# Two attentions and two feed-forward stages on one core: the first attention's last slab in pairs of slots, FFN products in the last batch's slots, a lead of three tiles

## The chip, the cores and the metric

The kernel runs on one core of a Trainium2 chip. The metric is the device time of one execution in microseconds (us). It is shown beside one profiled execution, whose trace gives every instruction's start and length on the engines: PE (TensorE, matmuls; PEld its weight loads), DVE (VectorE), ACT (ScalarE), POOL (GpSimd), and the DMA queues, of which SP (SyncE) issues most. TensorE's clock can be granted at less than full speed; the profile gives the granted share.

## The reference

For 4 batches of 256 tokens of width 256, with a context of 1601 tokens of width 128 per batch:

```
x = x + tanh(g_xattn[0]) * L0_xattn(layernorm(x), ctx)   # 16 heads of 16, q and k normed
x = x + tanh(g_ffn[0])   * L0_ffn(layernorm(x))          # shared expert + 8 of 16 routed
x = x + tanh(g_xattn[1]) * L1_xattn(layernorm(x), ctx)   # 16 heads of 128, 8 key heads
x = x + tanh(g_ffn[1])   * L1_ffn(layernorm(x))          # ternary weights, SiLU gate
```

The two parts that the change touches:

```
def L0_xattn(x, y):          # the last 16 context tokens attend apart and are added
    q = ln(x @ Wq + bq); k = ln(y_main @ Wk + bk); v = y_main @ Wv + bv
    ctx = softmax(q k^T / 4) v + softmax(q k_dca^T / 4) v_dca
    return ctx @ Wo + bo

def L0_ffn(x2):
    shared = x2 @ sw1.T * relu(x2 @ swg.T)**2 @ sw2.T
    xl = x2 @ Wdown.T                                     # the latent, width 64
    for e in range(16):
        ye = xl @ rw1[e].T * relu(xl @ rwg[e].T)**2 @ rw2[e].T
        acc += w_dense[:, e:e+1] * ye
    return shared + acc @ Wup.T
```

## The kernel before

The four stages run one after another; matmul outputs are [channels, tokens] or [keys, queries]. Within a stage a helper (`keep_order`) fixes every engine's order to the order in which the program records it, so the recorded order is the queue.

**First attention (lines 284 to 1247).** It works in *slabs* of one batch and four heads: 16 slabs, `u` from 0 to 15, four per batch. The four heads of a slab lie in four groups of 32 rows, so that a score matmul with 32 rows of contraction uses a quarter of PE's rows, and matmuls on different row groups run at the same time. A slab is cut into 14 *slots* (`SLOTS`): seven pairs of key tiles (the last has one tile), each once for the heads in row groups 0 and 1 and once for those in groups 2 and 3. A slot of `attend_tile` (L884) makes the scores of two heads for two key tiles (L894) into two PSUM banks, which ACT turns into exponentials (L904). After every odd slot `weigh` (L909, matmuls L918) multiplies the exponentials of two key tiles by the values.

Before a slab's scores its row maxima are needed. `greatest_tile` (L835) makes them from 14 tiles a slab: matmuls L849 into two banks of `ps_g`, DVE reductions L859 or L861. When the last of a slab's 14 is reduced, `shift` (L873 to L877) puts the maximum into the staged queries `qp`, and `turn_queries` (L803, transposes L807) turns them for the score matmuls. These tiles run ahead of the slots: one tile goes beside the scores in each slot, the list `ahead` starts one tile in front, and extra tiles at the slots in `CATCH_UP` (3, 5 and 7) bring the lead to four (`LEAD`). So the list ends in slot 205, and slots 206 to 223 have scores alone. The turn for the next slab is booked from slot 10 of a slab on, at odd slots in the first three batches and at even ones in the last.

PSUM has eight banks here: `ps_s` 3, `ps_g` 3, `ps_o` 1 (sums of `weigh`), `ps_m` 1. Everything else passes through `ps_m`: key and value projections, query projection, transposes, routing. `book` gives each such step a slot of its own, `chain` a row of slots, and `place` puts a step that needs no bank after a slot's work. Among them are the layernorm of the next batch (`plan_norm`, L1049; DVE L116 to L124, POOL L120), the projection, scaling and swap of the keys (`plan_keys`; the swap is three rounds of DMAs on SP, L643 to L649, for a pair of slabs), and in the last batch the routing of batches 0 to 2 (`route`, L203; matmuls L208 and L247).

**The opening loop (L1198 to L1215)** makes slab 0's maxima (seven steps `k`, two tiles each, four DVE reductions), beside the key projection of the second key set (steps 0 to 3, `key_project`: L522 into `ps_o`, activations L526 and L534), its roots (step 4: L557 into `ps_m`, DVE L564), and the value projection of batch 1, one pair of key tiles a step (`value_project`, L652: two matmuls L659, a copy by ACT L660).

**The end of the stage:** the last `weigh`, `take` (a copy by ACT), `put_heads` (transposes L940, DVE, POOL L949), `turn_heads` (L957), `out_project` (L965).

**First FFN (L1303 to L1480).** Tokens go in two halves of 512, two batches each. At its start `latent(0)` and `shared(0)` make the latent and the shared expert's products of the first half from `xnT` (`from_x`, matmuls L1383 with 256 columns; each 32-bit float matmul is two PE instructions). Then 32 experts follow (16 per half): `expert` (matmuls L1410, L1411, L1412 into `ps_v`, `ps_g`, `ps_w`), relu on ACT, products on DVE and POOL, `add_pair` (L1424). Between the experts stand other steps in `beside`: `latent(1)` at step 10 and `shared(1)` at step 13, and the preparation of the second attention. The slices of the tiles `scs` and `sq`, of 512 columns each, hold the results (`held`).

**Second attention and second FFN** follow (from L1487); the change leaves them as they are.

## Time and profile before

| | us |
|---|---|
| median of 3 runs (1486.24 to 1492.55) | 1489.6 |
| the profiled execution | 1492.74 |
| its span | 1491.0 |
| last matmul of `weigh` ends | 473.6 |
| first expert's matmul starts | 482.26 |
| first matmuls of the second attention on the chain | 583.45 |

Each row of the page's part 1 gives an engine's busy time, its share of the span and its instructions. The row of digits cuts the span in 40 slices of 37.3 us: PEclk is the clock that PE was granted in tenths, where 9 stands for 90% or more. Windows give, for a stretch of time, PE, PEld, DVE, ACT and POOL busy (with the count of instructions), then the granted clock, the DMA share and GB/s. The chain is the work that ended last, followed back from the end: start, length, engine, tile and line. Matmuls are pipelined, so lengths of single matmuls in the timeline overlap; the length of a group is what it took together.

Some further rows of the trace: the exponential L904 of 128 x 512 takes 571 ns on average, a reduction L859 624 ns and L861 621 ns. In all, PE waited 13.5 us for exponentials in the stretch from 88 to 440 us, and 2.8 us for the swap's DMA up to 90 us.

### The profile page before, as it was taken

To read this page: it belongs to the slowest core of one execution; us is meant where nothing else is said; L and a number is where in the kernel's file an instruction comes from. 1 tells how busy PE (TensorE), PEld (TensorE's weight loads), DVE (VectorE), ACT (ScalarE), POOL (GpSimd) and SP (SyncE) were. 2 spreads that over 40 slices of the span, in tenths; PEclk is the share of its full clock that TensorE was granted. 3 is DMA by queue.
4 is the path that set the end of the run, shared out by engine and by line. 5 is a ranking of instruction groups with operands and counts; after the bars stand their busy time and mean duration, and the time that the engine had idled before them with its cause. 6 is when DMAs were issued, how large, how long until landed. Compare 5 with 4: busy or idle time off the path is not lost.

```text
span 1491.0 us, 32194 instructions
## 1 busy us (share of the span) xinstructions
PE 1434.7 (96%) x12234; PEld 896.4 (60%) x12234; DVE 1081.6 (73%) x2556; ACT 802.9 (54%) x2055; POOL 641.5 (43%) x622
## 2 busy tenths in 40 slices
PE   7889999998999999799999999999999999999998
PEld 4455555555555444466666666666666666666677
DVE  6777787787761756877777777777877777877755
ACT  4467778687654344454444555444554444554433
POOL 4444463343321553444444444444444444445430
PEclk9799999999987999899999999999999999999999
DMA  5333422331212300000000000000000100000000
GB/s 136 45 53 65 65 48 32 56 57 35 62 44 62 134 1 1 2 9 10 16 16 16 9 10 16 16 9 9 10 17 9 23 9 16 10 2 2 2 1 29
DMA packets 63079, 43.47 MB, mean 29 GB/s; under 512 B 46474, under 2 KB 57100, under 8 KB 62796
## 3 DMA queue, kind: packets, MB, share of 16 engines
q1 hardware_dynamic: 48636, 39.66, 12.7%
q10 hardware_dynamic: 14288, 1.75, 0.7%
q8 instruction: 96, 1.57, 0.4%
q14 instruction: 59, 0.48, 0.1%
HBM read 32.67 MB, written 4.66 MB: 25 GB/s over the span
## 4 chain that ended last, share of the span: by engine, by line
PE 87%; DVE 5%; ACT 3%; POOL 2%; DMA 1%; issue 1%; SPq 0%; ACTq 0%; DVEq 0%; POOLq 0%
PE ps_o L1648 24%; PE ps_sc L1585 22%; PE ps_o L918 6%; PE ps_s L894 6%; PE ps_y L1666 4%; PE ps_m L1574 4%; PE ps_g L849 3%; PE ps_v L1410 2%; ACT e L904 2%; PE ps_m L659 1%; PE ps_m L522 1%; PE ps_a L1424 1%; DVE mxs L859 1%; PE ps_y L1826 1%; PE ps_g L1803 1%
## 5 line engine op out<-in xcount | busy, mean ns | idle before, releaser
L1635 POOL TENSOR_TENSOR pr<-pr,rs 128x1604 f32<-128x1604 f32 x128 | 364.0, 2866 | 443.6 <-DMA rs<-ws 379.1
L1648 PE MATMUL ps_o<-pT,cx 128*128 128x256 f32 x1664 | 372.0, 381 | 8.2 <-DVE pT L1641 8.2
L1592 DVE CUSTOM_DVE_ANT_0 pr<-ps_sc,mk 128x401 f32<-128x401 f32 x512 | 294.3, 576 | 92.9 <-PE ps_sc L1585 54.1
L1585 PE MATMUL ps_sc<-ctxT,qT 128*32 128x401 f32 x4096 | 359.5, 502 | 0.5 <-DVE nm L1592 0.5
L1600 ACT ACTIVATE pr<-pr,nm 128x401 f32<-128x401 f32 x512 | 321.2, 628 | 69.7 <-DVE nm L1592 69.0
L1648 PEld LDWEIGHTS ps_o<-pT,cx 128*128 128x128 f32 x1664 | 317.6, 191 | 52.8 <-DVE pT L1641 9.3
L904 ACT ACTIVATE e<-ps_s 128x512 f32<-128x512 f32 (+1 forms) x429 | 222.1, 571 | 103.0 <-PE ps_s L894 65.7
L859 DVE TENSOR_REDUCE mxs<-ps_g 128x1 f32<-128x454 f32 x372 | 216.8, 624 | 64.8 <-PE ps_s L894 40.0
L1585 PEld LDWEIGHTS ps_sc<-ctxT,qT 128*32 128x32 f32 x4096 | 126.2, 110 | 204.3 <-issue 118.3
L1641 DVE STREAM_TRANSPOSE pT<-pr 128x1664 f32<-128x1664 f32 x128 | 242.9, 1899 | 5.2 <-POOL pr L1635 5.2
L894 PE MATMUL ps_s<-qT,kS 32*128 32x256 f32 x1596 | 185.1, 319 | 16.0 <-ACT e L904 14.1
L894 PEld LDWEIGHTS ps_s<-qT,kS 32*128 32x128 f32 x1596 | 128.1, 192 | 95.1 <-ACT e L904 52.0
L849 PE MATMUL ps_g<-kS,qT 32*128 32x454 f32 (+1 forms) x960 | 160.1, 397 | 11.2 <-DVE mxs L861 4.3
L1617 ACT ACTIVATE ws<-ws 32x32 f32<-32x32 f32 x64 | 14.6, 228 | 201.5 <-DVE ws L1616 201.5
L918 PE MATMUL ps_o<-e,vp 128*32 128x256 f32 x1664 | 122.2, 409 | 0.0
L1658 ACT COPY ao<-ps_o 128x256 f32<-128x256 f32 x64 | 23.8, 372 | 151.5 <-PE ps_o L1648 136.4
L1600 ACT ACTIVATION_READ_ACCUMULATOR pr<-pr,nm 128x1 f32 x512 | 95.4, 186 | 0.0
L849 PEld LDWEIGHTS ps_g<-kS,qT 32*128 32x128 f32 x960 | 78.0, 188 | 18.4 <-DVE mxs L859 7.8
L1666 PE MATMUL ps_y<-vo,ao 128*128 128x256 f32 x256 | 72.2, 405 | 0.0
L1666 PEld LDWEIGHTS ps_y<-vo,ao 128*128 128x128 f32 x256 | 43.3, 189 | 43.9 <-ACT pr L1600 39.8
L918 PEld LDWEIGHTS ps_o<-e,vp 128*32 128x32 f32 x1664 | 44.9, 114 | 39.6 <-issue 14.7
L1614 DVE TENSOR_REDUCE low<-bq 32x8 f32<-32x32 f32 x64 | 12.4, 194 | 74.3 <-DMA bq<-nm 74.2
(346 smaller groups left out, 1632.3 us busy)
## 6 DMA issues: line engine op xcount, KB each, us to landing
scs<-by_row SPq DMA_DIRECT2D x56, 93.8 KB, 4.4
ctxT<-in_ctxT_dram SPq DMA_DIRECT2D x4, 800.5 KB, 8.2
held<-kS SPq DMA_DIRECT2D x32, 99.1 KB, 3.0
kS<-kS SPq DMA_DIRECT2D x32, 99.1 KB, 3.3
kS<-held SPq DMA_DIRECT2D x32, 99.1 KB, 3.6
ctx<-in_ctxT_dram SPq DMA_DIRECT2D x12, 200.0 KB, 4.2
kS<-in_L_xattn_Wq_dram SPq DMA_DIRECT2D x8, 256.0 KB, 5.0
wo<-in_L_xattn_Wo_dram SPq DMA_DIRECT2D x4, 512.0 KB, 4.7
```

The source lines that it names most:

```text
L849: nc.tensor.matmul(ps[:, m * w : (m + 1) * w], lhsT=part[rows, ii * P : (ii + 1) * P], rhs=kT[rows, n * CW0 : n * CW0 + w], start=part is ...
L859: nc.vector.tensor_reduce(mx[:, i, r + k, n : n + 1], ps[:, :w], AX.X, ALU.max)
L894: nc.tensor.matmul(ps[:, jj * S : (jj + 1) * S], lhsT=kT[rows, (j + jj) * P : (j + jj + 1) * P], rhs=part[rows], start=part is parts[0], s ...
L904: nc.scalar.activation(e[:, i, : nj * S], ps[:, : nj * S], AF.Exp)
L918: nc.tensor.matmul(summed[u][(r + k) * W : (r + k + 1) * W, :S], lhsT=vps[b % 2][:, t, h * VW : h * VW + W], rhs=made[u, j, r][:, k, jj * ...
L1585: nc.tensor.matmul(ps[i * TQ : (i + 1) * TQ, :KS], lhsT=queries[u][:, t * TQ : (t + 1) * TQ], rhs=ctxT[b][:, i * KS : (i + 1) * KS], start ...
L1592: nc.vector.tensor_tensor_reduce(out=prs[u % 3][:, t, :KS], in0=ps[:, :KS], in1=masks[b], scale=-1.0, scalar=3.0e38, op0=ALU.add, op1=ALU. ...
L1600: nc.scalar.activation(p, p, AF.Exp, bias=found[u][:, 0, t : t + 1], scale=-1.0, accum_out=found[u][:, 1, t : t + 1])
L1635: nc.gpsimd.tensor_tensor(p, p, bc_last(factors[:, ts], KS), ALU.mult)
L1641: nc.vector.transpose(pTs[u % 2][:, ts].rearrange("p t k -> p (t k)"), prs[u % 3][:, ts].rearrange("p t k -> p (t k)"))
L1648: nc.tensor.matmul(po[:, u % 2], lhsT=contexts[b][:, k, :], rhs=pTs[u % 2].rearrange("p t (k q) -> p t k q", q=TQ)[:, :, k, :], start=k == ...
L1666: nc.tensor.matmul(ys[b][:, i], lhsT=outs[u][:, i * P : (i + 1) * P], rhs=vo[:, h, :], start=(h, i) == (0, 0), stop=(h, i) == (H - 1, QT - 1),
```

## The change

1. *Scores in pairs of slots.* In the last slab the program records slots `k` and `k + 1` together, interleaved, so that four heads' matmuls stand side by side; the even slot's banks come from `ps_s`, the odd one's from `ps_g`. In the other slabs both banks are always from `ps_s` (before, slots with an empty `ahead` took one from each).
2. *FFN products.* `latent(b)` and `shared(b)` work on one batch, with 256 columns and one bank. For batches 0 to 2 they are booked into `ps_m` from slot 34 of the last batch on, at any parity, two slots apart; batch 3 stays in the FFN at steps 10 and 13. The relu and the product of `shared` go into the first two slices of `held`.
3. *Lead.* `LEAD` is 3, and the catch-up at slot 5 is gone: the tiles end in slot 206.
4. *Values of batch 1.* The opening loop makes none in steps 0 to 2, two pairs in each of steps 3 to 5, and the last in step 6; `ps_o` takes only the second pair of steps 4 and 5, all others `ps_m`.
5. *Norm of batch 1* is placed from slot 6 on instead of slot 0, and the query projection behind it moves along.

```diff
+    xlT, shT, held = {}, {}, []
+    def part_of(tiles, b):
+        if b // 2 not in tiles:
+            tiles[b // 2] = held.pop()
+        return tiles[b // 2][:, b % 2 * S : (b % 2 + 1) * S]
+    def latent(b, pl):
+        for c in range(DC):
+            nc.tensor.matmul(
+                pl[:, :S],
+                lhsT=fw["wdown"][:, c].rearrange("p i l -> p (i l)"),
+                rhs=xnT[b][:, c, :],
+                start=c == 0,
+                stop=c == DC - 1,
+            )
+        nc.scalar.copy(part_of(xlT, b), pl[:, :S])
+    def shared(b, ps):
+        pg, pv = ps[:, :S], ps[:, S:]
+        for dst, w in ((pg, fw["swg"]), (pv, fw["sw1"])):
+            for c in range(DC):
+                nc.tensor.matmul(dst, lhsT=w[:, c, :], rhs=xnT[b][:, c, :], start=c == 0, stop=c == DC - 1)
+        g, t1 = (t[:, b % 2 * S : (b % 2 + 1) * S] for t in held[:2])
+        nc.scalar.activation(g, pg, AF.Relu)
+        nc.vector.tensor_tensor(t1, pv, g, ALU.mult)
+        nc.gpsimd.tensor_tensor(part_of(shT, b), t1, g, ALU.mult)
...
-            pair = [bank(pool) for pool in ((ps_s, ps_s) if ahead else (ps_s, ps_g))]
+            pair = [bank(ps_g if u == len(slabs) - 1 and k % 2 else ps_s) for i in range(2)]
...
-            while slot in taken or slot % 2 != parity:
+            while slot in taken or parity is not None and slot % 2 != parity:
...
-        LEAD = 4
-        CATCH_UP = {3: 0, 5: 2, 7: 0}
+        LEAD = 3
+        CATCH_UP = {3: 0, 7: 0}
...
-            at = plan_norm(b, base)
+            at = plan_norm(b, base + 6 * (b == 1))
...
+        at = base + 34
+        for b in range(B - 1):
+            for step in (latent, shared):
+                at = book(at + 2, lambda b=b, step=step: step(b, bank(ps_m)), parity=None)
+        assert at < B * BATCH
...
-            value_project(1, VALUES[k], ps_o if k >= NG else None)
+            for t0 in VALUES[max(0, 2 * k - 6) : max(0, 2 * k - 4)]:
+                value_project(1, t0, ps_o if k >= NG and t0 % 4 else None)
...
-                several = [attend_tile(u, k)]
                 at = u * SLOTS + k
-                if ahead:
-                    several.append(next_greatest(ahead.pop(0), 2 - TILES[k][2]))
-                together(*several)
+                if u < len(slabs) - 1:
+                    several = [attend_tile(u, k)]
+                    if ahead:
+                        several.append(next_greatest(ahead.pop(0), 2 - TILES[k][2]))
+                    together(*several)
+                elif k % 2 == 0:
+                    together(attend_tile(u, k), attend_tile(u, k + 1))
...
-        beside.setdefault(10, []).append(lambda: latent(1))
-        beside.setdefault(13, []).append(lambda: shared(1))
+        beside.setdefault(10, []).append(lambda: latent(B - 1, ps_x.tile([P, 512], F32, name="ps_x")))
+        beside.setdefault(13, []).append(lambda: shared(B - 1, ps_x.tile([P, 512], F32, name="ps_x")))
...
-        latent(0)
-        shared(0)
```

In the recorded order of PE the six moved products stand behind slots 205, 207, 209, 211, 213 and 215, most of them right after the `weigh` of that slot. Behind the last `weigh` PE's queue goes on with the first expert's scores, the transposes of `put_heads`, the rest of the first expert and the start of the second, `turn_heads`, and `out_project`.

More of the change, by code (lines that the diff above doesn't have):

```diff
@@ L299, in tile_gated_cross_blocks @@
         sq = ktp.tile([P, NG * KG], F32, name="sq")
+        held.extend(t[:, k * 512 : (k + 1) * 512] for t in (scs, sq) for k in range(3))
         def open_raw(n):
@@ L1324, in tile_gated_cross_blocks @@
             nc.gpsimd.memset(ctxT[b][:, S2:], 0.0)
-        sw1, swg, sw2, wdown, wup, rwv, rw2, sel, wT = (
-            fw[n] for n in ("sw1", "swg", "sw2", "wdown", "wup", "rwv", "rw2", "sel", "wT")
-        )
+        sw2, wup, rwv, rw2, sel, wT = (fw[n] for n in ("sw2", "wup", "rwv", "rw2", "sel", "wT"))
         ep = ph.enter_context(tc.tile_pool(name="ep", bufs=2))
-        held = [t[:, k * 512 : (k + 1) * 512] for t in (scs, sq) for k in range(3)]
         ps_h = ph.enter_context(tc.tile_pool(name="f0ps_h", bufs=2, space=PSUM))
@@ L1376, in tile_gated_cross_blocks @@
         HB = HALF // S
-        xlT, shT, accT, sums = {}, {}, {}, {}
-        def from_x(half, ps, w, m):
-            for k in range(HB):
-                for c in range(DC):
-                    nc.tensor.matmul(
-                        ps[:m, k * S : (k + 1) * S],
-                        lhsT=w[:, c, :],
-                        rhs=xnT[half * HB + k][:, c, :],
-                        start=c == 0,
-                        stop=c == DC - 1,
-                    )
-        def latent(half):
-            pl = ps_h.tile([P, 512], F32, name="ps_v")
-            from_x(half, pl, wdown.rearrange("p c i l -> p c (i l)"), 2 * LAT)
-            xlT[half] = held.pop()
-            nc.scalar.copy(xlT[half], pl)
-        def shared(half):
-            pv = ps_h.tile([P, 512], F32, name="ps_v")
-            pg = ps_h.tile([P, 512], F32, name="ps_g")
-            from_x(half, pv, sw1, HID)
-            from_x(half, pg, swg, HID)
-            shT[half] = held.pop()
-            squared_relu_times(shT[half], pg, pv)
+        accT, sums = {}, {}
         def expert(half, e):
```

## The prediction

> **What bounds the kernel now.** I read the page first (shares, the 40 slices, the granted clock), then windows of 10 us, then the chain of waits, then the timeline around the places that the change touches.
>
> ```profile
> span 1491.0 us, 32194 instructions
> PE 1434.7 (96%) x12234; PEld 896.4 (60%) x12234; DVE 1081.6 (73%) x2556; ACT 802.9 (54%) x2055; POOL 641.5 (43%) x622
> PEclk9799999999987999899999999999999999999999
> ```
>
> TensorE is the bound, with two dips of its clock, in slice 1 and in slices 11 and 12: the start and the end of the first attention. The windows (PE, weight loads, DVE, ACT, POOL, then the granted clock) show both:
>
> ```profile
> 50.00:60.00 10.00, 8.51 (x58) 5.25 (x58) 8.12 (x16) 6.44 (x12) 4.13 (x10) 0.50 0.57 53
> 60.00:70.00 10.00, 9.53 (x81) 4.67 (x78) 5.19 (x9) 4.84 (x10) 4.54 (x7) 0.71 0.01 2
> 440.00:450.00 10.00, 10.00 (x73) 5.56 (x69) 0.89 (x6) 3.99 (x10) 4.14 (x8) 0.50 0.01 2
> 450.00:460.00 10.00, 10.00 (x78) 6.63 (x82) 2.70 (x15) 5.90 (x13) 1.12 (x5) 0.50 0.00 0
> 490.00:500.00 10.00, 10.00 (x49) 4.32 (x50) 6.70 (x12) 3.93 (x9) 6.15 (x9) 1.00 0.76 315
> ```
>
> Narrow windows put the half clock at 48.8 to 65.8, 82.9 to 86.3, 414.0 to 417.3 and 437.9 to 468.6 us: always whole steps of 3.41 us. Each start follows a step with some 1.2 us or more of idle PE; each end follows a step with PE fully busy on instructions that fill all its rows. In 440 to 460 PE is never idle and still stays at half: there most score matmuls use two of the four 32-row groups. A step at half clock does 1.93/1.07 = 1.8 times less work (L918's rows below), so it costs 3.41 x (1 - 1/1.8) = 1.5 us.
>
> Chain of waits (start, length, work):
>
> ```profile
> 39.81 2.23 DVE mxs L859 x4
> 56.44 2.29 DVE xn L124 x2
> 78.28 3.55 DMA kS<-kS
> 471.38 2.21 PE ps_o L918 x24
> 478.37 1.80 PE ps_m L965 x8
> 480.60 1.74 PE ps_g L1383 x8
> 518.58 1.73 PE ps_v L1383 x8
> ```
>
> The FFN's products from x (L1383) lie on the chain on both sides of the stage boundary, 8 instructions in 1.73 us: 0.217 us each. Timeline, full and half clock, and one turn of queries:
>
> ```profile
> 459.77 1.93 PE L918 MATMUL ps_o<-e,vp 128*32 128x256 f32 x16
> 469.62 1.07 PE L918 MATMUL ps_o<-e,vp 128*32 128x256 f32 x16
> 385.72 1.16 DVE L861 TENSOR_REDUCE mxs<-ps_g 128x2 f32<-128x448 f32 x2 [0.29 <-PE ps_g L849]
> 387.41 0.25 DVE L877 TENSOR_TENSOR qp<-qc,mx 128x8 f32<-128x8 f32 x2
> 387.71 0.44 PE L807 MATMUL ps_m<-ident,qp 128*128 128x128 f32 x2 [0.39 <-DVE qp L877]
> ```
>
> **1. FFN products moved.** A batch has 12 such instructions (4 latent, 8 shared), 48 in all; 36 move to slots 205 to 215 of the first attention. Around the boundary the chain goes last L918 (ends 473.6), heads, L957, L965 (ends 480.2), L1383 until 482.3. The 6.6 us to L965's end stay. After them 2.2 us of L1383 go; and in the new PE order the scores of experts 0 and 1 stand in the gaps that L1383 filled: two experts took 482.26 to 485.44, all but the last 0.5 us of which can slide under: 2.6. Gain 4.8, bounds 2.2 (the experts wait for DVE instead) and 5.2 (all 24 instructions). Further on, the second half's 24 L1383 (5.2 us) are halved where PE is busy 10 of 10: 2.6, at least 1.3 should DVE (6.7) or POOL (6.2) end last. Sum: 7.4, bounds 3.5 to 7.8. Their copies, relus and products go along; in the FFN those engines have slack.
>
> **2. The last slots.** Before: 438.5 (L918 after slot 205) to 473.6, 35.1 us. After, at full clock: eight L918 groups of 1.07, one of 0.57, the last 1.6 = 10.8; score pairs at 0.69 (slots 220 and 221, 468.93 to 469.62) six times, 0.4 for the last, 2.3 for slots 206 to 209 = 6.8; transposes and routing 2.4; moved products 36 x 0.217 = 7.8. Together 27.8. "Side by side" itself is small: PE already runs neighbouring slots together when nothing stands between them (slots 212 and 213 start at 453.82 and 453.85); only three pairs are newly joined. Added waits: the greatest tile that ended in slot 205 now ends in slot 206, and the query turn right behind it waits for its reductions and the shift (439.57 minus 438.41, then 0.7): 1.9. ps_m has one buffer: the routing and shared products wait for evacuations queued behind exponentials, about 1.5. In the last three pairs ACT needs 4 x 0.545 = 2.2 against PE's 1.76, with final exponentials behind: about 1.5. Sum 32.7: gain 2.4, 5.5 with no wait but the turn's.
>
> The clock decides the worse bound. At half clock for the whole stretch, by L918's 1.93, pairs of 1.2 (453.82 to 455.0) and 0.43 per product, it is 19.3 + 12 + 4.1 + 15.6 + 1.9 = 53: 18 lost. I take full clock, with the products filling all rows.
>
> [...]
>
> Slot 205's scores now leave ps_g alone, so the greatest tile there needn't wait (PE was busy 1.86 of 3.41 us in 434.7 to 438.1): gain 1.0, bounds 0 and 1.4.
>
> **3. Lead of three.** A greatest tile ends one slot later; in the last four slabs the turn L807 follows at once. In slot 178 L807 came at 387.71 behind tile 177's shift. Now tile 178's (PE until 387.3, 1.2 of reductions, 0.75 of shift) ends at 389.35: 1.6 late. Slot 192, likewise: 1.2. Behind L807 PE's scores queue, then ACT's exponentials. Loss 2.8; bounds 0 and 6, with a further 3.41 us step at half clock each. In earlier slabs the turn is a slot later and an L918 group (1.0) covers it.
>
> For it, the catch-up tile of slot 5 goes (66.78 to 67.45): 0.7. The swap that PE waits for at 78.3 to 82.0 (2.8 us in all) is wanted one slot (1.9) later, though POOL now does the late norm's 0.72 ahead of it: gain 1.5, bounds 0 and 2.8.
>
> **4. Value products of batch 1.** Before, one pair per step of the opening loop; steps are 2.7 us, on PE. Now none in steps 0 to 2, then two pairs each. Steps 0 to 2 fall to DVE's 2.3: 1.6 gained by step 3. In step 3 both pairs take the single ps_m: the second waits for two activations and a copy (0.58 + 0.67 + 0.58). In step 4 the pair behind L557 waits until DVE has reduced the step and read the roots; in step 5 it waits for the queries' copy. DVE, the bound there (9.77 of 10 in 40 to 50), idles meanwhile: step 6 starts 4.3 after its 44.42. Loss 4.2, net of the 1.6; bounds 0 and 5.
>
> **5. Norm of batch 1, six slots later.** L124's 2.29 and 1.3 of statistics leave the DVE queue of slots 1 to 3, where PE waited 0.93 for DVE. Gain 1.0, bounds 0 and 2.3. With no such gaps a step fills up sooner and the half clock there (17 us, five steps) can end earlier: each step saves 1.5. I take two: 3.0, bounds 0 and 5 (ACT and DVE need 1.9 a slot at any clock).
>
> **Sum.** -7.4 - 2.4 - 1.0 + 2.8 - 0.7 - 1.5 + 4.2 - 1.0 - 3.0 = -10.0 us. The profiled execution took 1492.74 (span 1491.0 and 1.74 around it), 3.1 above the runs' median of 1489.6. On its own time: 1482.7; on the median: 1479.6, which I say.
>
> **Rivals.**
> - The opening takes it back: value products cost their 4.2, the half clock there stays five steps, two of the three turns trigger a further step each. For it: DVE at 9.77 of 10, and that idle of 1.2 us was enough at 414.0. Against it: fewer DVE waits in slots 1 to 3. -10.0 + 3.0 + 3.0 = -4: 1485.6, no measurable change (below 0.5%, 7.4 us, I call it the same).
> - The half clock holds through the last slots: place, slots 206 to 223; price up to 18 + 2.4. For it: the turn's 1.9 us idle, and 30 us at half before with a PE busy throughout. Against it: products and pairs fill all rows, as in the step that ended it (465.2 to 468.6). -10.0 + 20.4 = +10.4: 1500, slower. That is 20.4 over 53/3.41 = 15.5 steps, 1.3 each: it decides from about eight steps on.
> - The scoring does nothing new, since PE already paired slots: then only its 3 newly joined pairs (0.6 each) and the 1.0 of part 2 go: 1482.4.
> - Better: both half clocks shrink to a step each, and nothing but the turns waits: -10.0 - 2.0 (part 5 at its bound) - 3.1 (part 2 at its) = -15.1: 1474.5.
>
> Chances: forecast, with the scoring rival beside it, 0.45; better 0.12; opening 0.30; half clock 0.13. Below 1482.2 lie the better case and most of the first: faster 0.54; same 0.33; slower 0.13. Range 1470 to 1491: it leaves out the half-clock case and the far end of the better one.
>
> **What would show it.** L1383's successors sit before the last L918; the first expert's scores start within 1 us of it. Clock 1.00 in most of the last slots. The opening's step 6 starts near 48.7, not 44.4. L807's successor waits 1 to 2 us on DVE three times, in slots 178, 192 and 206. PE idle before the kS swap shrinks to about 1 us. I am wrong if the clock falls in the last slots for eight steps, or if the opening's delay isn't made up by slot 14.

## The result and the profile after

The changed kernel is slower. In the first comparison it took 1503.88 us (median of 5 runs, 1498.28 to 1505.49) against 1489.6 before: a ratio of 1.0092, 95% interval 1.0066 to 1.0117. Compared again it took 1497.84 against 1486.99: 1.0079 (1.0049 to 1.0108). The profiled execution took 1504.13 us, with a span of 1502.4 against 1491.0. The forecast was 1479.6.

In the profile after, `turn_queries` writes from L836 (L807 before), `greatest_tile` from L878 with its reductions on L888 and L890 (L849, L859, L861), `attend_tile` from L923 (L894), `weigh` from L947 (L918), `out_project` from L994 (L965). The moved products are L199 (latent) and L212 (shared); the experts are L1419 to L1421 (L1410 to L1412).

The page of the changed kernel:

```profile
span 1502.4 us, 32196 instructions
PE 1435.3 (96%) x12234; PEld 897.4 (60%) x12234; DVE 1082.2 (72%) x2558; ACT 803.1 (53%) x2059; POOL 641.6 (43%) x624
PEclk9899999999898999899999999999999999999999
```

TensorE is busy for the same time as before (1435.3 against 1434.7), and the mean granted clock of the two profiled executions is the same (0.977 and 0.978), so the page alone shows only that 11 us more passed without work. The windows of the changed kernel (length, then PE, weight loads, DVE, ACT, POOL, granted clock, DMA share, GB/s) show the places:

```profile
390.00:400.00 10.00, 8.94 (x93) 5.27 (x94) 5.52 (x11) 3.81 (x9) 3.59 (x5) 0.83 0.01 2
400.00:410.00 10.00, 9.36 (x96) 5.60 (x93) 6.25 (x12) 5.73 (x12) 1.60 (x6) 0.61 0.01 2
440.00:450.00 10.00, 8.97 (x95) 5.51 (x91) 8.26 (x26) 4.67 (x10) 3.06 (x6) 0.83 0.01 2
450.00:460.00 10.00, 7.90 (x52) 4.78 (x50) 1.76 (x6) 2.92 (x6) 2.19 (x7) 0.67 0.01 2
490.00:500.00 10.00, 6.89 (x25) 3.06 (x25) 6.89 (x15) 2.85 (x5) 4.09 (x9) 0.89 0.48 149
500.00:510.00 10.00, 8.84 (x35) 3.35 (x35) 5.11 (x8) 2.08 (x5) 4.42 (x4) 0.77 1.01 375
```

Before, 440 to 460 had a full PE at clock 0.50; now the clock there is higher but PE has gaps, and half clock has appeared in two places that were at 1.00 before: 390 to 410, and the boundary to the FFN, 490 to 510. The chain of waits of the changed kernel goes through both (start, length, work):

```profile
390.35 0.44 PE ps_m L836 x2
391.45 1.39 PE ps_o L947 x16
...
403.86 1.86 PE ps_o L947 x16
...
422.28 0.44 PE ps_m L836 x2
...
453.03 0.41 PE ps_m L836 x2
...
456.45 3.73 PE ps_m L212 x8
...
484.76 1.87 PE ps_o L947 x24
486.63 1.05 PE ps_v L1419 x2
...
491.72 1.94 PE ps_m L994 x8
...
496.53 2.44 POOL hT L1408 x2
...
499.67 1.35 DVE xn L124
501.16 0.66 PE ps_x L135 x2
```

L836 is there three times, as L807 was before (387.71, 413.32, 441.48), but 2.6, 9.0 and 11.6 us later. Behind the first, weighing (L947) takes 1.39 and then 1.86 us, where it takes 1.00 at full clock. Shared products took 3.73 us for 8, twice the 1.73 that they took in the FFN. Behind the first expert (L1419) the chain no longer goes through PE: POOL's products and DVE's norm (L124) set when L135 starts. The timeline of the changed kernel gives the waits (start, length, engine, work, then in brackets the idle time and what ended it):

```profile
390.35 0.44 PE L836 MATMUL ps_m<-ident,qp 128*128 128x128 f32 x2 [2.09 <-DVE qp L906]
422.28 0.44 PE L836 MATMUL ps_m<-ident,qp 128*128 128x128 f32 x2 [1.94 <-DVE qp L906]
453.03 0.41 PE L836 MATMUL ps_m<-ident,qp 128*128 128x128 f32 x2 [2.10 <-DVE qp L906]
501.16 0.66 PE L135 MATMUL ps_x<-ident,xn 128*128 128x128 f32 x2 [2.06 <-DVE xn L124]
```

Before, the second turn and the norm's transposes had waited less (the first turn's 0.39 stands in the prediction, the third turn had no such wait):

```profile
413.32 0.44 PE L807 MATMUL ps_m<-ident,qp 128*128 128x128 f32 x2 [0.56 <-DVE qp L877]
489.97 0.44 PE L135 MATMUL ps_x<-ident,xn 128*128 128x128 f32 x2 [0.55 <-DVE xn L124]
```

The opening loop of the changed kernel has waits for value products that the kernel before has not, for the copy of the pair before (ACT) and for the roots (DVE):

```profile
38.57 1.13 PE L688 MATMUL ps_m<-wv,ctx 128*128 128x256 f32 x4 [0.85 <-ACT vp L689]
43.16 1.13 PE L688 MATMUL ps_m<-wv,ctx 128*128 128x256 f32 x4 [1.66 <-DVE r_v L593]
```

A ruler for all that follows is the take of a slab (ACT's copy of ps_o into oT, once a slab, 0 to 15). In each cell stands the length of the stretch in one profiled execution and, behind the stroke, how much of it the clock record has at 0.50 (us); the second attention is taken to begin at 585.11 us before, 595.25 in the changed kernel. The last three rows are experiments told of below.

| kernel | to take 0 | take 0 to 11 | take 11 to 14 | take 14 to 15 | take 15 to 2nd attention | rest |
|---|---|---|---|---|---|---|
| before | 94.6 / 20.5 | 279.6 / 0 | 79.8 / 19.5 | 19.6 / 14.6 | 111.5 / 0 | 905.9 / 12.0 |
| changed | 93.7 / 17.1 | 281.4 / 3.4 | 91.5 / 27.3 | 20.1 / 3.4 | 108.6 / 6.8 | 907.1 / 11.4 |
| late_turn | 93.3 / 17.1 | 282.8 / 6.8 | 75.9 / 0 | 19.7 / 0 | 109.9 / 6.8 | 906.2 / 8.9 |
| late_fill_h | 93.9 / 17.1 | 279.8 / 0 | 78.8 / 10.2 | 17.0 / 0 | 107.1 / 0 | 906.7 / 11.6 |
| lead_late_pairs | 85.5 / 6.8 | 285.1 / 13.7 | 78.6 / 20.5 | 14.1 / 0 | 111.5 / 0 | 907.0 / 11.3 |

Read against before, the changed kernel has lost nothing up to take 0, 11.7 us between takes 11 and 14 (where the three turns stand, and the first of the moved products), and has gained 2.9 in the FFN. Of the 11.7, PE's idle time is 5.7 (12.0 against 6.3); the rest is moved work and the slower clock.

### The profile page after: what moved, and what is told of

Same layout as the page of the kernel before. It is cut to its first block, busy times and chain, and to the rows that moved or that the text cites. A ratio compares the mean times of both kernels' runs of the same rounds, so it can differ in the third digit from the quotient of the medians.

```text
span 1502.4 us, 32196 instructions
## 1 busy us (share of the span) xinstructions
PE 1435.3 (96%) x12234; PEld 897.4 (60%) x12234; DVE 1082.2 (72%) x2558; ACT 803.1 (53%) x2059; POOL 641.6 (43%) x624
## 4 chain that ended last, share of the span: by engine, by line
PE 87%; DVE 5%; ACT 4%; POOL 2%; issue 1%; DMA 0%; ACTq 0%; DVEq 0%; SPq 0%; POOLq 0%
PE ps_o L1655 23%; PE ps_sc L1592 22%; PE ps_s L923 6%; PE ps_o L947 6%; PE ps_y L1673 4%; PE ps_g L878 4%; PE ps_m L1581 4%; PE ps_v L1419 2%; ACT e L933 2%; PE ps_m L688 1%; PE ps_a L1433 1%; PE ps_m L551 1%; PE ps_y L1833 1%; DVE mxs L890 1%; PE ps_g L1810 1%
## 5 line engine op out<-in xcount | busy, mean ns | idle before, releaser
L933 ACT ACTIVATE e<-ps_s 128x512 f32<-128x512 f32 x434 | 223.4, 570 | 94.1 <-PE ps_s L923 69.4
L888 DVE TENSOR_REDUCE mxs<-ps_g 128x1 f32<-128x454 f32 x372 | 216.8, 624 | 70.9 <-PE ps_s L923 47.8
L923 PE MATMUL ps_s<-qT,kS 32*128 32x256 f32 x1612 | 180.2, 319 | 17.0 <-ACT e L933 15.7
L923 PEld LDWEIGHTS ps_s<-qT,kS 32*128 32x128 f32 x1612 | 124.9, 192 | 94.1 <-ACT e L933 53.4
L878 PE MATMUL ps_g<-kS,qT 32*128 32x454 f32 (+1 forms) x960 | 160.3, 402 | 6.4 <-DVE mxs L888 3.4
L1624 ACT ACTIVATE ws<-ws 32x32 f32<-32x32 f32 x64 | 14.6, 228 | 202.1 <-DVE ws L1623 197.5
L947 PE MATMUL ps_o<-e,vp 128*32 128x256 f32 x1664 | 119.4, 403 | 0.0
L878 PEld LDWEIGHTS ps_g<-kS,qT 32*128 32x128 f32 x960 | 78.1, 191 | 11.7 <-DVE mxs L888 7.1
L850 POOL CAST qT<-qT 128x256 fp32r<-128x256 f32 x30 | 12.3, 410 | 132.5 <-ACT qT L849 132.3
L947 PEld LDWEIGHTS ps_o<-e,vp 128*32 128x32 f32 x1664 | 44.6, 113 | 37.3 <-issue 11.7
```

The costliest lines, as they stand in the source:

```text
L878: nc.tensor.matmul(ps[:, m * w : (m + 1) * w], lhsT=part[rows, ii * P : (ii + 1) * P], rhs=kT[rows, n * CW0 : n * CW0 + w], start=part is ...
L888: nc.vector.tensor_reduce(mx[:, i, r + k, n : n + 1], ps[:, :w], AX.X, ALU.max)
L923: nc.tensor.matmul(ps[:, jj * S : (jj + 1) * S], lhsT=kT[rows, (j + jj) * P : (j + jj + 1) * P], rhs=part[rows], start=part is parts[0], s ...
L933: nc.scalar.activation(e[:, i, : nj * S], ps[:, : nj * S], AF.Exp)
L947: nc.tensor.matmul(summed[u][(r + k) * W : (r + k + 1) * W, :S], lhsT=vps[b % 2][:, t, h * VW : h * VW + W], rhs=made[u, j, r][:, k, jj * ...
```

## The experiments

Theories before the first runs: L, the lead of three makes the three turns wait, and each wait brings half clock with it; F, the moved FFN products are the cost; P, the joined pairs; O, the opening.

One thing has to be known to read the times. The executions of one kernel differ, and they differ with the granted clock. The 137 executions of the kernel before that ran beside these experiments have spans from 1475.8 us (clock 0.992) to 1493.6; within a kernel, over all of them, the span falls by 1.10 us for each 0.001 of clock (a common slope fitted to all executions). So the table gives, beside the measured ratio, the mean granted clock and the mean span moved along that slope to a clock of 0.983. The last column shows work and waits (standard errors 0.1 to 0.4 us, 1.0 for no_pairs with its four executions); the clock column shows what the granted clock added. A difference of two mean clocks has a standard error of 0.001 to 0.002, so most of those differences are not clear of noise one by one. The intervals of the ratios hold both.

| kernel | edit | ratio to before (95%) | mean clock | span at 0.983 |
|---|---|---|---|---|
| before | | 1 | 0.9816 | 1485.3 |
| changed | all | 1.0092 (1.0066 to 1.0117), 1.0079 (1.0049 to 1.0108) | 0.9795 | 1495.7 |
| no_lead | changed, lead of four | 1.0091 (1.0068 to 1.0114) | 0.9805 | 1496.6 |
| no_ffn | changed, no moved products | 1.0045 (1.0021 to 1.0068) | 0.9813 | 1490.4 |
| no_pairs | changed, no joined pairs | 1.0116 (1.0067 to 1.0165) | 0.9785 | 1496.4 |
| old_open | changed, old opening | 1.0029 (1.0010 to 1.0048) | 0.9813 | 1489.2 |
| old_values | changed, old values, late norm | 1.0069 (1.0043 to 1.0095) | 0.9784 | 1490.9 |
| late_turn | changed, turns later | 1.0021 (0.9996 to 1.0046) | 0.9849 | 1492.1 |
| open_late | changed, old opening, turns later | 1.0000 (0.9980 to 1.0021) | 0.9822 | 1486.6 |
| late_fill | late_turn, batch 2 back (ps_x) | 1.0021 (0.9995 to 1.0046) | 0.9836 | 1491.3 |
| open_late_fill | open_late, the same | 0.9980 (0.9960 to 1.0000) | 0.9838 | 1486.0 |
| late_fill_h | late_turn, batch 2 back (ps_v, ps_g) | 1.0003 (0.9974 to 1.0032) | 0.9852 | 1488.8 |
| only_lead | before, lead of three | 1.0004 (0.9983 to 1.0025) | 0.9810 | 1485.9 |
| lead_late | before, lead of three, turns later | 1.0003 (0.9974 to 1.0032) | 0.9791 | 1482.5 |
| only_pairs | before, joined pairs | 0.9983 (0.9960 to 1.0005) | 0.9850 | 1484.8 |
| lead_pairs | before, lead of three, pairs | 0.9978 (0.9954 to 1.0002) | 0.9836 | 1485.2 |
| lead_late_pairs | the same, turns later | 0.9931 (0.9904 to 0.9958), 0.9949 (0.9924 to 0.9975) | 0.9847 | 1480.6 |
| late_pairs_norm | the same, late norm | 0.9963 (0.9939 to 0.9988) | 0.9828 | 1481.4 |

### One part taken out at a time

no_lead:

```diff
-        LEAD = 3
-        CATCH_UP = {3: 0, 7: 0}
+        LEAD = 4
+        CATCH_UP = {3: 0, 5: 2, 7: 0}
```

> The changed kernel with the lead back at four tiles and the catch-up tile of slot 5 restored; the rest of the change stays. Theory L (the turns of slots 178, 192 and 206 wait on DVE for 1.9 to 2.1 us each and each idle puts a half-clock step behind it): the 7.2 us lost between slots 178 and 205 come back whole, and 2 to 4 of the last slots' 5.0; the swap's 1.5 and the catch-up's 0.7 are lost again: about 1496, and the three turns wait under 0.6 us. Theory F (the moved FFN products are what costs): only the three stalls themselves come back, 3.1 us: about 1501, with the last slots still near 40 us.

1.0091, 1500.5 us: the time did not move, and it is F's figure, not L's. The turns waited 0.39 and 0.56 us again and takes 11 to 14 took 83.6 us instead of 91.5, as L says; but take 0 came at 99.5 instead of 93.7, and take 2 at 156.6 instead of 144.1, with three more steps at half clock on the way. L had the place right and had put what the lead gains in the opening at 2.2 us, when it was 5.8 by take 0 in these two profiles.

no_ffn (the products computed at the FFN's start, as before):

```diff
-        at = base + 34
-        for b in range(B - 1):
-            for step in (latent, shared):
-                at = book(at + 2, lambda b=b, step=step: step(b, bank(ps_m)), parity=None)
...
+        latent(0)
+        shared(0)
```

> The changed kernel with the FFN's latent and shared products back at the start of the FFN and none in the first attention's slots. Theory F: the last slots lose the products' 36 x 0.217 = 7.8 us at full clock or 15.6 at half, some 10 us, and the FFN gives back its measured 2.9: about 1497. Theory L: TensorE does the same work elsewhere, 7.8 us less here and 7.4 us more there: 1503, and the 7.2 us lost in slots 178 to 205 stay.

1.0045, so F was nearer: the moved products cost 5.3 us at equal clock (6.0 and 4.0 in two other pairs of kernels below). From take 14 to 15 it took 15.2 us against 20.1; the FFN took 113.1 against 108.6. Moving them costs more than it brings.

no_pairs (the last slab's scores slot by slot):

```diff
-            pair = [bank(ps_g if u == len(slabs) - 1 and k % 2 else ps_s) for i in range(2)]
+            pair = [bank(pool) for pool in ((ps_s, ps_s) if ahead else (ps_s, ps_g))]
...
-                elif k % 2 == 0:
-                    together(attend_tile(u, k), attend_tile(u, k + 1))
```

> The changed kernel with the last slab's score pairs slot by slot on ps_s, as before. Theory P (the joined pairs bring the bank and ACT waits of the last slots): 3 us come back, about 1501. Theories L and F: pairing was worth 1 to 2 us, so about 1505, with the turns' waits as they were.

1.0116 from four executions. The interval of the ratio holds both figures; at equal clock no_pairs is 0.7 us slower than the changed kernel (standard error 1.1), where P wanted it 3 faster: P falls.

old_open:

```diff
-            at = plan_norm(b, base + 6 * (b == 1))
+            at = plan_norm(b, base)
...
-            for t0 in VALUES[max(0, 2 * k - 6) : max(0, 2 * k - 4)]:
-                value_project(1, t0, ps_o if k >= NG and t0 % 4 else None)
+            value_project(1, VALUES[k], ps_o if k >= NG else None)
```

> The changed kernel with one value product pair per step of the opening loop and batch 1's norm at its old place, as before. Theory O (the opening's 4.5 us are what costs): 4 us come back, about 1500, with slot 17 reached 4 us earlier. Theories L and F: the opening had repaid itself by slot 17 (0.9 us ahead of before), so it costs 1 us more: about 1505.

1.0029, better than even O had said, and 6.5 us at equal clock. The first exponential came at 51.0 instead of 55.4 and take 0 at 88.0 instead of 93.7. That the opening "had repaid itself" was a wrong reading: the lead had paid for it. At equal clock the new opening is the dearest part of the change (6.5; 5.5 with the late turn).

### The turns

late_turn:

```diff
-                book(at + 10, lambda u=u: turn_queries(u + 1, 1), parity=odd)
+                book(at + 10 + 2 * (1 - odd), lambda u=u: turn_queries(u + 1, 1), parity=odd)
```

> The changed kernel with one edit: in the last batch the turn of the next slab's queries is booked two slots later, behind the slot whose weighing covers DVE's reductions and shift. Theory L (the turns' waits of 2.09, 1.94 and 2.10 us and the half-clock steps behind them): the three waits vanish; of the 11.7 us that the changed kernel lost between the take of slab 11 and that of slab 14 some 8 come back, so 1.0037 of before, 1495. Rival C (the clock falls there anyway, from the waits for ACT's exponentials, 0.71 and 0.64 us, at each slab's end): only the stalls net of the 0.39, 0.56 and 0 before come back, 5 us: 1.0058, 1498.

1.0021, a little better than L expected; C falls. Of the 12 to 14 us that the changed kernel loses (1.0079 to 1.0092) 9 to 10 went with this one edit. Its turns in the timeline, and its windows over the stretch that held 27.3 us of half clock:

```profile
393.43 0.44 PE L836 MATMUL ps_m<-ident,qp 128*128 128x128 f32 x2
...
419.28 0.44 PE L836 MATMUL ps_m<-ident,qp 128*128 128x128 f32 x2
...
446.16 0.44 PE L836 MATMUL ps_m<-ident,qp 128*128 128x128 f32 x2 [0.49 <-DVE scs L215]
```

```profile
395.00:405.00 10.00, 8.11 (x114) 4.80 (x106) 6.97 (x14) 6.12 (x13) 2.40 (x7) 1.00 0.01 2
405.00:415.00 10.00, 8.74 (x129) 5.43 (x126) 9.28 (x20) 6.21 (x12) 3.59 (x4) 1.00 0.01 2
445.00:455.00 10.00, 7.73 (x82) 4.68 (x80) 0.79 (x2) 5.44 (x15) 2.92 (x8) 1.00 0.00 0
```

No turn waits for the shift (L906) any more, and the clock stays at 1.00 throughout, though PE is idle for 1.9 and 2.3 us in two of these windows: waits of 0.64 and 0.74 us for ACT's exponentials and one of 1.63 for the routing's copy are left, and here no half clock lies behind them. At equal clock the edit is worth 3.6 us, and its mean clock is 0.0054 higher (standard error 0.0016): 5.4 x 1.10 = 5.9 us.

Only the first of these two numbers comes back elsewhere. The late turn is in three more pairs of kernels below: at equal clock it is worth 2.6, 3.4 and 4.6 us there, but the mean clock moves by +0.0009, -0.0019 and +0.0011. In the profiles with the late turn the half clock between takes 11 and 14 is 0 to 20.5 us, with the early turn and a lead of three 13.7 to 33.1. So the waits' own price is shown four times; that half clock follows from them is seen in this pair alone.

only_lead and lead_late (on the kernel before; CATCH_UP goes along with the lead):

```diff
-        LEAD = 4
-        CATCH_UP = {3: 0, 5: 2, 7: 0}
+        LEAD = 3
+        CATCH_UP = {3: 0, 7: 0}
```

> The kernel before with only the lead of three tiles (no catch-up tile in slot 5) and the late turn: no moved products, no joined pairs, the old opening. Theory: the lead alone brings the 6.5 us that the changed kernel with the old opening had gained at the take of slab 0, since nothing else of the change acts there, and without the turns' waits none of it is lost: 0.9956, 1481. Rival (those 6.5 us come of the clock's luck in one execution, and the swap is simply waited for elsewhere): 0.9985 to 1.000.

> The kernel before with the lead of three (no catch-up tile in slot 5) and nothing else. Theory L: by itself it does both things, the opening's gain (6 us by the take of slab 0, as in the run with the late turn) and the three turns' waits of about 2 us with half-clock steps behind them, so 8 us more than with the late turn: 1.0055 of before, 1495. Rival (the turns cost only because the moved products and joined pairs stand behind them): no more than the stalls, 1.001 to 1.003.

Both came out level with before, 1.0003 and 1.0004, close to the rival's figures each time. The traces show the theory's parts all the same: take 0 came 6.0 and 9.4 us earlier than before, takes 13 to 14 took 25.3 us with the late turn and 29.9 without. At equal clock the late turn is worth 3.4 us here (1485.9 and 1482.5), and the lead without the waits gains 2.8. The clock hid both: lead_late has a mean of 0.9791, and in its profile the last slots are at half clock for 23.9 us (30.7 before).

lead_pairs has the lead and the pairs, with the turns where they were:

> Lead of three and joined pairs on the kernel before, with the turns at their old slots. Theory L (the turns' waits cost by themselves, 4.5 us of idle plus some half-clock steps of 1.5): 8 us more than with the late turn (0.9931), so 0.9985. Rival N (the price of the turns comes only with the moved products behind them, as the run with the lead alone suggests): 0.993 to 0.995.

0.9978, near L's 0.9985 and not N's 0.993 to 0.995: against the same kernel with the late turn (1480.6) the waits cost 4.6 us at equal clock, without any moved product near them.

### The opening and the combinations

open_late (old_open's edit and late_turn's):

> The changed kernel with the opening loop's value products and batch 1's norm as before, and the late turn. Theory: the two costs are in different places and add: 1.0029 as measured without the new opening, less 8 us for the turns: 0.9975, 1483.7. Rival (what the opening gains is lost to the next wait, the clock included): 1.000 to 1.003.

1.0000, the lower end of the rival's range. At equal clock the edits nearly add (9.1 us below the changed kernel, of 6.5 and 3.6; 5.5 below late_turn, 2.6 below old_open), but the mean clock fell from 0.9849 to 0.9822, which gives 3.0 us of it back.

old_values, the old value products with the late norm:

> The changed kernel with only the value products back to one pair per step of the opening loop; batch 1's norm stays six slots later. It splits the 6 us that the new opening cost: if the values are the cost (4.2 us up to the first attend, one more half-clock step), 1.003, as without both; if the norm's shift is the cost, 1.008 to 1.009.

1.0069, between the two theories. At equal clock old_values is 4.8 us faster than the changed kernel and 1.7 slower than old_open: most of the opening's cost is the value products', and the norm's shift gains nothing. The same shift on the best version, with the gain of the best version itself run again:

> The fastest version so far (lead of three, late turn, joined pairs; no moved products, old opening) once more on another chip: 0.993 to 0.995 of before if the gain is its own, 0.997 or more if it was the clock's luck in six executions.

> The same with batch 1's norm six slots later, the part of the change that has not been seen by itself. By the prediction's step 5 (1.0 us of DVE's queue and up to two half-clock steps, 4.0 in all) 0.0027 below the run beside it; by the runs with old and new values (1.0069 with the late norm, 1.0029 without it) up to 0.004 above; no difference if those two differ only by where the clock's steps fell.

0.9949 and 0.9963, overlapping, 0.8 us at equal clock the wrong way (1.7 between old_values and old_open): step 5 of the prediction brings no gain that can be measured.

### The FFN's boundary

late_fill puts batch 2's products back, late_fill_h does it in other PSUM tiles:

```diff
-        for b in range(B - 1):
+        for b in range(B - 2):
             for step in (latent, shared):
                 at = book(at + 2, lambda b=b, step=step: step(b, bank(ps_m)), parity=None)
...
+        for step in (latent, shared):
+            step(B - 2, ps_x.tile([P, 512], F32, name="ps_x"))
```

```diff
-        for step in (latent, shared):
-            step(B - 2, ps_x.tile([P, 512], F32, name="ps_x"))
+        for step, name in ((latent, "ps_v"), (shared, "ps_g")):
+            step(B - 2, ps_h.tile([P, 512], F32, name=name))
```

> The changed kernel with the late turn, and the latent and shared products of batch 2 back at the start of the FFN; those of batches 0 and 1 stay moved. Theory B (the FFN gave back what it had gained because TensorE ran ahead of DVE's late norm: 3.1 us idle in 490 to 500, then 6.8 us at half clock): the 12 products, 2.6 us, cover that wait, the stretch from the last take to the second attention falls from 109.9 to about 106 to 107.5 with no half-clock step behind the boundary, and the last slots lose 2.6: 5 us in all, 0.9988, 1485. Rival (the idle is only pushed on to the next DVE result): that stretch stays at 109 to 110 and the time at 1.000 to 1.002.

> The same with the old opening as well (value products one pair per step, norm at its old place). If opening, turns and boundary add: 1.000 as measured with old opening and late turn, less 5: 0.9966, 1482. If the clock gives it back elsewhere: 0.999 to 1.001.

late_fill came to 1.0021, no better than late_turn, with the stretch behind take 15 at 113.8 us instead of 109.9. The norm's wait did fall from 2.06 to 0.55, but the timeline of late_fill has new ones:

```profile
471.00 0.80 PE L986 MATMUL ps_m<-ident,heads 128*128 128x128 f32 x4 [1.97 <-POOL heads L978]
472.48 3.78 PE L994 MATMUL ps_m<-w_wo,aoT 128*128 128x256 f32 x8 [0.68 <-ACT aoT L988]
477.11 2.08 PE L199 MATMUL ps_x<-xnT,kk 128*128 128x256 f32 x4 [0.85 <-DVE aoT L996]
```

L199 waits for DVE's reading (L996) of the output projection's tile: this tile of ps_x takes a bank that ps_m still held, so (read from the wait and the pools, not tested apart) the products could not run beside the heads, nor could the experts queued behind them. PE stood idle and L994 ran at half clock (3.78 against 1.94). In late_fill_h they are written to the experts' tiles, and its timeline shows them at the place where the kernel before had them:

> The changed kernel with the late turn and batch 2's latent and shared products at the FFN's start, now in the PSUM tiles of the experts (ps_v, ps_g), as the kernel before had them, and not in ps_x, whose bank was still held by the output projection. Theory B (the FFN gave back its gain because TensorE ran ahead of DVE's late norm): products stand in the gaps of the heads' turn again, the norm's wait stays at 0.55 us, no half-clock step follows; the stretch from the last take to the second attention is 106 to 108 (109.9 with the late turn alone), the last slots 17.0: 0.9985 of before. Rival (the boundary has no cover to give, the experts fill it already): that stretch 110 or more, 1.001.

```profile
469.36 1.13 PE L199 MATMUL ps_v<-xnT,kk 128*128 128x256 f32 x4
470.32 0.38 PE L969 MATMUL ps_m<-ident,oT 128*128 128x128 f32 x2
470.54 1.46 PE L212 MATMUL ps_g<-xnT,kk 128*128 128x256 f32 x6
472.67 0.66 PE L986 MATMUL ps_m<-ident,heads 128*128 128x128 f32 x4 [0.67 <-POOL heads L978]
...
484.06 0.41 PE L135 MATMUL ps_x<-ident,xn 128*128 128x128 f32 x2 [0.64 <-DVE xn L124]
```

The stretch took 107.1 us with no half clock, the last slots 17.0, both as theory B said; the time fell by 3.3 us at equal clock (1488.8 against 1492.1), to 1.0003 where 0.9985 was expected (the interval holds both). open_late_fill, 0.9980 where 0.9966 was expected, has the bad tiles and gained in the last slots what it lost in the FFN (17.0 and 113.9).

This is the one place where the half clock comes with the edit every time. In all eight profiles of kernels with the products of three batches moved, L135 waits 2.06 to 2.27 us and 6.8 us at half clock lie beside that wait. In the nine without moved products it waits 0.55, and seven have no half clock there, two have 3.4. Two steps in an execution of 1486 us are 0.0023 of mean clock; the three pairs of kernels with and without the products differ by 0.0018, 0.0025 and 0.0023 (standard errors 0.0012 to 0.0015).

### The pairs, and a version that beats both

only_pairs (the two hunks of no_pairs, on the kernel before):

> The kernel before with the last slab's joined pairs alone, lead of four. Theory P2 (pairs over all four row groups bring the full clock back in the last slots): the stretch from the take of slab 14 to that of 15 falls from 19.6 to about 14.5, 0.9965 of before. Rival (a lucky clock in the profiled execution of the run with late turn and pairs): stays near 19 to 20, 0.999 to 1.001.

lead_late_pairs:

> Lead of three, late turn and the last slab's joined pairs on the kernel before; no moved products, old opening. Theory P2 (pairs over all four row groups bring the full clock back in the last slots without any product beside them: 15.2 us from the take of slab 14 to that of 15 in the changed kernel without moved products, against 21.1 with the late turn alone, 14.4 of them at half clock): 5.5 us off, 0.9965, 1482. Rival (the products are what restores the clock): those slots stay at 20 to 21 us, ratio 1.000.

In both the stretch from take 14 to 15 is 13.8 and 14.1 us, all at full clock, with no product in it. The first window below is of lead_late, which has neither pairs nor products, the second of only_pairs:

```profile
450.00:460.00 10.00, 10.00 (x74) 6.68 (x70) 2.25 (x14) 4.95 (x11) 0.00 (x0) 0.50 0.00 0
```

```profile
450.00:460.00 10.00, 9.32 (x145) 5.26 (x141) 0.69 (x3) 9.16 (x20) 1.12 (x5) 1.00 0.01 2
```

145 instructions against 74 in the same 10 us. only_lead shows that the half clock was no certainty without pairs: the same slots as lead_late's, unpaired, ran in 14.3 us in its profile. Of the four unpaired profiles two have some 14 us at half clock from take 14 to 15 and two 0 and 1.8; none of the sixteen paired ones has more than 4.5. At equal clock the pairs are worth 0.5 to 1.9 us (1485.3 to 1484.8, 1482.5 to 1480.6); the rest of what they bring is the clock, 0.0034 and 0.0056 higher in the mean.

lead_late_pairs is faster than both kernels: 0.9931 (6 executions) and, on another chip, 0.9949 of before (12). Its page:

```profile
span 1481.8 us, 32188 instructions
PE 1427.8 (96%) x12234; PEld 893.9 (60%) x12234; DVE 1080.5 (73%) x2556; ACT 801.8 (54%) x2055; POOL 642.2 (43%) x622
PEclk9999999998799999899999999999999999999999
```

open_late is this version with the moved products: they cost 6.0 us at equal clock, and by the ratios 0.5 to 0.7%. Likewise old_open is lead_pairs with the products: 4.0 us.

after_again, the changed kernel once more, was to show how much one kernel varies:

> The changed kernel once more, on the chip of the three runs beside it. 1.009 of before; waits of the three turns again 2.1, 1.9 and 2.1 us; the places of the half-clock steps may differ, since they follow a grid that has no fixed place in the program.

1.0079, the waits 2.09, 1.94 and 2.10 us to the hundredth, but half clock at 352.9 (10.2 us) and 380.2 (13.7 us), where the first profile had none. Within each of the profiles of before and changed all starts and ends of half clock lie whole multiples of 3.41 us apart, but the first start is at 48.77 us in the one and at 54.01 in the other.

## Why the prediction was wrong

It said -10.0 us; the profiled executions differ by +11.4. Three of its steps carry the miss.

**The clock in the last slots and behind the turns (parts 2 and 3).** What failed is the choice "I take full clock". Part 2 said 32.7 us for the stretch behind slot 205, a gain of 2.4. It took 40.1 (446.49 to 486.63), a loss of 5.0: PE was idle for 4.2 us where 4.9 was forecast, but 13.7 us, four steps, were at half clock where the sum had none. The same slots in late_turn, all at full clock, took 33.7, so at full clock the sum was right to 1 us. The windows of these slots, of before, changed, late_turn and only_pairs in turn:

```profile
438.40:473.60 35.20, 35.20 (x306) 19.95 (x305) 5.10 (x25) 19.65 (x43) 5.26 (x13) 0.57 0.04 5
446.49:486.63 40.14, 35.92 (x350) 21.92 (x349) 9.04 (x34) 21.71 (x49) 7.45 (x16) 0.83 0.02 3
438.03:471.70 33.67, 29.91 (x353) 18.46 (x349) 9.36 (x39) 21.62 (x49) 7.38 (x16) 1.00 0.02 4
435.98:461.20 25.22, 23.04 (x306) 13.23 (x305) 5.10 (x25) 19.31 (x43) 5.25 (x13) 0.95 0.04 5
```

The other side of the same step is the 35.1 us that the last slots were to improve on: 30.7 of them were at half clock, some 13 us of loss at the prediction's price, and the forecast spent that on the 7.8 us of products. Without products, and with all but 2.4 us at full clock, only_pairs ran these slots in 25.2. The slow stretch was that of one execution: its clock was 0.978, the mean over 137 executions is 0.9816, some 4 us by the slope, and over three quarters of them lie above 0.978. Over all executions the change made the mean clock worse (0.9795), 2.3 us, where the prediction counted on a gain. As an estimate: nine steps at its 1.5 us here and the 3.0 us of part 5 are 16.5 of clock in the forecast's sum; without them it says +6.5, against 10.4 at equal clock.

The three turns' waits were forecast at their places and almost to the tenth: L836 came 1.6 us late and waits of 1.9 were named; the idle was 2.09, 1.94 and 2.10, and the equal-clock price of the early turn, 2.6 to 4.6 us, does not pass the 2.8 + 1.9 of the sum. A half-clock step behind each was put only into the bound of 6; the stretch had 27.3 us at half clock against 19.5 before. How much of that the waits bring is open: with late_turn 9 to 10 us came back by the ratio, in the other three pairs 0 to 7.

**The FFN's 7.4 (part 1).** 2.9 us came. The edit was costed by the chain before, in which L1383 stood before the experts, and DVE's waits (0.65 us then) were taken as covered. Without 24 of those matmuls in front, PE reached the norm's turn (L135) before DVE had written xn: 2.06 us of idle in place of 0.55, 2.2 at the experts in place of 1.5, and 6.8 us of half clock beside these waits. From the last take to the second attention PE's busy time fell by 5.2 us (108.73 to 103.50), not by the 7.8 that moved out, and its idle time rose by 2.3 (2.75 to 5.08). late_fill_h supports this: with 12 products given back, both the idle and the half clock were gone. The range's lower bound, 3.5 us, did not reach it, though it named a wait for DVE at this place. Behind it lies a plainer point: both stages are bound by PE, so 7.8 us of matmul moved from one to the other gains only what idle it fills, and the boundary had 2.7. In the last slots the products cost about their whole length: 33.7 us in late_turn against only_pairs' 25.2.

**The opening (parts 4 and 5).** The value products cost what was said: first attend 4.1 us late against 4.2. The sum of -2.0 for everything up to the first slabs was met as well (-0.9 at take 0, -2.0 at take 3). Inside it two terms are wrong and cancel, which is luck: the norm's shift, -1.0 - 3.0, has no gain; the lead, -0.7 - 1.5, brings 4.6 to 9.4 by take 0 with the old opening, in eight profiles, by how many half-clock steps fall there (two to six, where before had six). Over the whole kernel at equal clock, without the turns' waits, the lead brings 2.8 to 4.5.

**Right:** the joined pairs as a small gain at equal clock; the idle of the last slots (above); the swap's wait gone from the chain. Of the rivals, "the half clock holds through the last slots" came out at the right time, 1500, but with four steps there (three in the second profile), half of the eight from which it was to decide; at equal clock the loss is elsewhere.

**Open:** why half clock comes behind short waits in one execution and not in another. In the changed kernel's profile it began at 272.46 us, after 3.41 us in which PE was idle for 0.70; in the profile before PE was idle for 0.71 us in 345.7 to 349.1 and for 1.00 in 362.8 to 366.2, and the clock was 1.00 throughout. In the stretch from take 0 to 11, where the change moves almost nothing, the profiles have between 0 and 13.7 us at half clock.

The parts can be read along one row of kernels that ran, at equal clock: before 1485.3, with the lead 1485.9 (its gain less the turns' waits), with the pairs 1485.2, with the products 1489.2, with the new opening 1495.7. So of the 10.4 us the products make 4.0 and the opening 6.5; in other company the products cost up to 6.0 and the opening 5.2 to 5.5.

## What to carry to other kernels

Here 7.8 us of work, moved from one stage to another in which the same engine is the bound, had 2.7 us of idle to gain at the boundary and cost 4.0 to 6.0 us at equal clock; look for what it was covering where it stood, as the norm on DVE was covered here. The turns' three waits of some 2 us cost 2.6 to 4.6 us together at equal clock, no more than their length; half clock lay beside the wait of 2.06 to 2.27 us at the FFN's boundary each time (6.8 us in eight profiles), and around the turns in changing amounts (13.7 to 33.1 us between takes 11 and 14 with the waits, 0 to 20.5 without). A later place for the waiting instruction was the cheaper one in all four pairs (by those 2.6 to 4.6 us). Before a stretch at half clock is counted as a loss that can be recovered, see how the clock of other executions stands: the 30 us of the profile before were not in every execution (the fastest, at a mean clock of 0.992, can have had no more than 24 us at half clock in all, an estimate: 2 x 0.008 x 1476).

## What the runs showed of the hardware

- Half clock came in whole steps of 3.41 us in every profile (3.4, 6.8, 10.2, 13.7, 17.1, 20.5, 23.9, 30.7 us), but for the stretch that runs into the end of the execution. By the fitted slope a step costs, as an estimate, 1.10 x 3.41 / (2 x 1.486) = 1.26 us of span, where the prediction used 1.5.
- The same instructions in the last slots ran in 14.3 us in one profile (only_lead) and in 21.1 in another (lead_late, 14.2 of it at half clock, PE busy 10.00 of 10). PE stayed at half clock with next to no idle time: for 30.7 us before (busy 35.20 of 35.20 us from 438.4), for 23.9 in lead_late (busy 9.55 of 10.00 us from 440, 20.00 of 20.00 from 450). In both most score matmuls there use two of four row groups; that this is the reason is not shown.
- The clock differs where the program does not: two profiles of one and the same kernel (the changed one) had 3.4 and 13.7 us at half clock between takes 0 and 11.
